# The last attention layer's end: a closing's sum on GpSimd, one row in PSUM, and the last tiles bank by bank

## The chip, the cores and the metric

The kernel runs on one core of a Trainium2 chip. The metric is the device time of one execution, in microseconds. Before the change the median of three runs is 3555.47 us (3555.02 to 3556.88).

Five engines work side by side, each with its own queue: TensorE (PE; its weight loads are listed as PEld), VectorE (DVE), ScalarE (ACT), GpSimd (POOL) and SyncE (SP), which here issues DMAs. PE writes to PSUM; the others work on SBUF, and VectorE and ScalarE on PSUM too.

## The reference

Two graph layers run over `x` (8 batches, 2048 nodes, 256 features) with one 0/1 adjacency matrix. Each is wrapped as `x = layernorm(x + layer(x))`.

```python
# layer 0: per batch, 4 heads of 64; keys in 8 chunks of 256, softmax within a chunk
scores = clip(q @ k / 8, -10, 10); scores = where(adj == 0, -10, scores)
ctx = sum over chunks of softmax(scores) @ v
out = layernorm(ctx @ Wo + bo + x) * gamma + beta
# layer 1: per batch, 4 heads of 64
Wh = h @ W
e = leaky_relu(s_src[i] + s_dst[j], 0.2); e = where(adj, e, -inf)
h_out = elu(softmax(e over j) @ Wh)
```

For layer 1 the kernel uses `max` of two products in place of the exponential of a leaky relu: a tile is `e = max(row_i, gd_j) * edge_ij`, and its product with the values `waug` gives the weighted sums and, in one more column, the denominator. A closing divides by the denominator, applies `elu`, adds the residual and normalizes.

## The kernel before

**Tiling.** All is fp32. Layer 1 of one batch is 128 tiles: 8 units (2 halves of the nodes by 4 heads) of 16 tiles, each tile 128 source nodes by 1024 target nodes. A tile is made by `make` (one VectorE operation, L927) and used by `use` (32 recorded matmuls, L964, into the two PSUM banks of `pa`). For a unit in the last batch with an odd number, both banks of `pa` are one tile, `psA2`.

**Stages.** Layer 1 of batch b runs alongside layer 0 of batch b+1. Two stretches differ. In the *join*, the list `order` at the end of the last batch's loop, the last 20 tiles of batch 6's layer 1 (the held tiles) stand between the last projections of batch 7; the list is written by hand, and each engine gets its queue in that order. `M` is a make, `U` a use, `R` a step of a closing. `b2` and `group.a` are normalizations of the second to last and the last quarter of the nodes; `fs` are four steps that prepare the factors and rows of the next layer 1. `two_banks` hands out three pairs of PSUM banks (`psA0` to `psA2`) in turn.

In the *last layer*, layer 1 of batch 7 runs alone (`self.alone`), 64 steps of two tiles. Every third tile (`by_pool`) is prepared by two ScalarE operations (L888, L889) and one GpSimd product (L890), up to 8 tiles ahead (`make_ahead`); the other two by VectorE. The row that VectorE reads is copied to PSUM by ScalarE (`lift`, L856). A held row still lies in SBUF (`srow`).

**Closings.** When a unit's last tile is used, ScalarE copies `pa` to `raw` (L986), and `close` is stepped along in the following steps: denominators on VectorE (L1005, L1008), the division on GpSimd in the last layer and for the last two units of batch 6 (L1013), Exp and Relu on ScalarE (L1024, L1025), and the sum `min(exp, 1) + relu` on VectorE (L1029), which writes `h1`. The residual of quarters whose heads are all closed is added by GpSimd (L1067, and L1086 for three heads of the last two quarters), VectorE takes statistics (L545, L548), GpSimd raises to the power -0.5 (L556), ScalarE applies (L594).

**The end.** The last unit has no such closing. `Close.last` is a generator of three parts for each of the two last quarters: division, Exp and residual (L1092 to L1099); sum and statistics (L1103, L545); application, alternately on ScalarE and VectorE (L1115, L1118), and the store. The loop at the end steps both generators in turn. For the last `LAST` = 4 tiles the products of bank 0 come first, and those of bank 1 after the fourth tile.

Of the kernel before, what the change touches and what calls it, by code (L numbers as in the profile page):

```python
# [8 lines left out]
F32 = mybir.dt.float32  # L9
# [4 lines left out]
AF = mybir.ActivationFunctionType  # L14
ALU = mybir.AluOpType
AX = mybir.AxisListType

P = 128
# [4 lines left out]
def adj_resnorm_kernel(  # L23
# [19 lines left out]
    nc = tc.nc  # L43
    B, N, F = x.shape
    H, D = a_src.shape
    NT = N // P
    NCH = N // CH
# [24 lines left out]
    UNITS = [(m, h) for m in range(len(BANKS)) for h in range(H)]  # L72
    FIRST = [sum(BANKS[:m]) for m in range(len(BANKS))]
# [3 lines left out]
    WIDE = max(BANKS)  # L77
    AHEAD_E = 5
    AHEAD_P = 8
    ROOMS_P = 5  # L80
    LAST = 4
    n_banks = WIDE // QT
    assert TILES == STEP * SLOTS and NT % 2 == 0 and all(n == WIDE for n in BANKS)

# [8 lines left out]
    psA = ctx.enter_context(tc.tile_pool(name="psA", bufs=1, space=bass.MemoryType.PSUM))  # L93
# [12 lines left out]
        )  # L106
    )

    turn_of, bank_of = [0], [0]

    def two_banks(shape, name):

        turn_of[0] = (turn_of[0] + 1) % 3
        return psA.tile(shape, F32, tag=f"psA{turn_of[0]}", name=name)

    def one_bank(shape, name, kind=F32):

# [6 lines left out]
    h1 = big.tile([P, NT, F], F32, tag="h1", name="h1")  # L124
# [165 lines left out]
    def by_node(dram, b, g):  # L290

        return dram[b, g * CH : (g + 1) * CH, :].rearrange("(t p) f -> p t f", p=P)
# [310 lines left out]
    class Between:  # L603
# [86 lines left out]
    every = tuple(range(QT))  # L690
# [5 lines left out]
    MIDDLE_OF = {  # L696
        1: lambda o: o.bias(),
        5: lambda o: o.g == 0 and o.shift(),
        6: lambda o: o.a.factors(),
        7: lambda o: o.scale(),  # L700
    }
# [9 lines left out]
    NEXT_MIDDLE = {  # L711
        0: lambda o: o.again(),
        3: lambda o: o.b2.factors(),
        4: lambda o: o.load(),
        5: lambda o: o.turn(),
    }
# [80 lines left out]
    class Layer1:  # L797
# [41 lines left out]
        def load_row(self, n):  # L839
            if n < len(UNITS):  # L840
# [9 lines left out]
                )  # L850
                self.rows[n] = srow

        def lift(self, n):
            if n < len(UNITS):
                self.lifted[n] = psA.tile([P, WIDE * P], F32, tag=f"psA{n % 2}", name="rowp")
                nc.scalar.copy(self.lifted[n], self.rows[n])  # L856
# [80 lines left out]
        def use(self):  # L937
# [34 lines left out]

            if self.alone and k >= TILES - LAST:

# [19 lines left out]
        def close(self, u, raw, pas):  # L994
            m, h = UNITS[u]
            n = BANKS[m]

            wide = self.alone and u < len(UNITS) - 2
            if wide:
                yield 1  # L1000
            dn = small.tile([P, n, 1], F32, tag="dn", name="dn")
            if self.alone:
                for i, pa in enumerate(pas):
                    k = slice(i * QT, (i + 1) * QT)
                    nc.vector.tensor_scalar(dn[:, k, :], pa[:, :, D:D1], 1e-30, None, ALU.max)  # L1005
            else:
                nc.vector.tensor_scalar(dn, raw[:, :, D:D1], 1e-30, None, ALU.max)
            nc.vector.reciprocal(dn, dn)  # L1008
            yield 1
            by_pool = self.alone or (self.b == B - 2 and u > len(UNITS) - 3)  # L1010
            if by_pool:
                v = raw[:, :, :D]
                nc.gpsimd.tensor_mul(v, v, dn.to_broadcast([P, n, D]))  # L1013
            for k in range(n):
                if k == n // 2:
                    yield 1
                if not by_pool:
                    v = raw[:, k, :D]
                    nc.scalar.activation(v, v, AF.Copy, scale=dn[:, k, :])  # L1019
            yield 1  # L1020

            ee = small.tile([P, n, D], F32, tag="ee", name="ee")
            hp = raw[:, :, :D]
            nc.scalar.activation(ee, hp, AF.Exp)  # L1024
            nc.scalar.activation(hp, hp, AF.Relu)  # L1025
            yield 1
            if wide:
                yield 1
            nc.vector.scalar_tensor_tensor(  # L1029
                h1[:, FIRST[m] : FIRST[m] + n, h * D : (h + 1) * D],  # L1030
                ee,
                1.0,
                hp,
                op0=ALU.min,
                op1=ALU.add,
            )

        def step(self):
            self.rest(1 + (len(self.tail) > 1))
# [4 lines left out]
    class Close:  # L1044
# [43 lines left out]
        def last(self, pa):  # L1088

            f = slice((H - 1) * D, F)  # L1090
            dn = small.tile([P, QT, 1], F32, tag="dn", name="dn")
            nc.vector.tensor_scalar(dn, pa[:, :, D:D1], 1e-30, None, ALU.max)  # L1092
            nc.vector.reciprocal(dn, dn)
            hh = small.tile([P, QT, D], F32, tag="raw", name="hh")
            nc.vector.tensor_mul(hh, pa[:, :, :D], dn.to_broadcast([P, QT, D]))
            ee = small.tile([P, QT, D], F32, tag="ee", name="ee")
            nc.scalar.activation(ee, hh, AF.Exp)
            hp = small.tile([P, QT, D], F32, tag="acc", name="hp")
            nc.vector.scalar_tensor_tensor(  # L1099
                hp, hh, 0.0, self.x[:, :, f], op0=ALU.max, op1=ALU.add  # L1100
            )
            yield 1
            nc.vector.scalar_tensor_tensor(  # L1103
                self.h[:, :, f], ee, 1.0, hp, op0=ALU.min, op1=ALU.add
            )
            self.n = Norm(self.h, "c")
            self.n.stats(tuple(range(QT)))
            yield 1
            o = self.x
            to = by_node(out, self.b, self.g)  # L1110
            for k in range(QT):
                rs, off = self.n.rs[:, k : k + 1], self.n.off[:, k : k + 1]
                src, dst = self.h[:, k, :], o[:, k, :]
                if k % 2:
                    nc.vector.tensor_scalar(dst, src, rs, off, ALU.mult, ALU.add)  # L1115
                    nc.sync.dma_start(out=to[:, k - 1 : k + 1, :], in_=o[:, k - 1 : k + 1, :])
                else:
                    nc.scalar.activation(dst, src, AF.Identity, bias=off, scale=rs)  # L1118

    HOME = (blocks, "xb", 2)  # L1120
    HOME_Y = (blocks, "y", 2)
# [38 lines left out]
    for g in range(NCH):  # L1160
        _, _, keys, values, queries = groups[g]
# [67 lines left out]
    lower = None  # L1229
    for b in range(B):  # L1230
# [8 lines left out]
        group = before = None  # L1239
        for p in range(PAIRS):  # L1240
# [22 lines left out]
            def hook(now, later):  # L1263
                if group and i in now:
                    now[i](group)
                if before and i in later:
                    later[i](before)
# [3 lines left out]
            if i == 0 and q:  # L1271
                before, group = group, Between(b, q - 1, sd, waug)
# [31 lines left out]
            if ending:  # L1304
                last.bias()
                lower.room = prp, "pr"
            hook(MIDDLE_OF, NEXT_MIDDLE)
            for each in closings:
                each.do(p, "add", "factors")
            if i == 2 and q:  # L1310
# [57 lines left out]
        before = group  # L1368
        gd, fs = factors(b, sd, waug)
        group = None  # L1370
# [8 lines left out]
        coming = Layer1(b, gd, waug)  # L1379
# [33 lines left out]
        if b + 1 < B:  # L1413
            (k0, v0, q0), (l1, t1, k1, v1, q1), (l2, t2, k2, v2, q2), (l3, t3, k3, v3, q3) = turns
            rest = [lambda: lower.rest(1)] if lower else []
            order = [begin, early[0], *rest, l1, k0, ctx, early[2], v0, steps[0], *rest, steps[1], t1, l2, *rest]
            order += [q0, steps[2], early[3], steps[3], l3, k1, *rest, steps[4], v1, early[4], t2, q1]
            order += [steps[5], k2, steps[6], early[5], early[6], steps[7], coming.begin, v2, t3]
            order += [lambda: [load_slab(p) for p in range(2)], steps[8], steps[9]]
            order += [lambda: k3(fs[0]), fs[1], lambda: q2(fs[2]), coming.start, v3, start_next]  # L1420
            order += [lambda: [exps(*us) for us in units_of(0)], q3, coming.make, coming.make]
        else:


            M, U, R = lower.make, lower.use, lambda: lower.rest(1)
            b2 = lambda: before.b2
            order = [begin, U, U, U, ctx, before.again, M, U, lambda: b2().sums(every), steps[1], M]
            order += [lambda: b2().squares(every), lambda: b2().factors(nc.gpsimd), steps[2]]
            order += [lambda: group.a.stats(every), U, U, U, early[2], M, U, M, U, steps[4], before.turn_all]
            order += [lambda: coming.load_masks(0), group_shift, M, U, early[5], early[6], steps[5]]  # L1430
            order += [M, U, R, M, U, R, steps[6], M, U, M, steps[7], U, R, M, M, steps[8], R, M, U, R, M, M]
            order += [steps[9], U, U, fs[0], U, fs[1], fs[2], U, lambda: coming.start(fs[4])]
            assert sum(p is U for p in order) + 1 == LATE * STEP
            assert sum(p is M for p in order) + 2 + 5 >= LATE * STEP
        for piece in order:
# [4 lines left out]
        lower = coming  # L1440
# [17 lines left out]
            each.do(s, "load", "pool", "stats", "most", "finish")  # L1458
    send()
    ends = [ending.of[2 + k].last(pa) for k, pa in enumerate(lower.pa)]  # L1460
    for _ in range(3):
        for end in ends:
            next(end, None)


# [40 lines left out]
```

## Time and profile before

| what | us |
|---|---|
| median of three runs | 3555.47 |
| the profiled execution, its own time | 3554.9 |
| its span, first to last instruction | 3553.1 |
| PE, VectorE, ScalarE, GpSimd busy in the span | 3496.8, 3033.1, 2306.8, 1426.0 |
| first tile of the last layer on PE | 3396.57 |
| last matmul ends | 3539.34 |
| PE busy after 3395, and idle between its instructions | 126.0, 16.8 |

The span is cut from the first to the last instruction; the own time has 1.8 us more around it. A row of a timeline gives start, duration, engine, line, operation, `out<-in`, shapes and a count of equal instructions that follow each other; in square brackets stands how long the engine had been idle, and on what it waited. The mean granted clock of PE is 0.997 of full speed.

### The profile page before, as it was taken

How to read it: one execution, taken by the hardware profiler on the slowest of the kernel's cores; microseconds unless marked ns; L12 is line 12 of the kernel's file. 1: busy time of each engine (PE TensorE's matmuls, PEld its weight loads, DVE VectorE, ACT ScalarE, POOL GpSimd, SP SyncE). 2: the span in 40 equal slices, each digit the busy share in tenths (PEclk: the TensorE clock that was granted, in tenths of full speed). 3: DMA queues.
4: the chain of work that ended last, by engine and by line, in shares of the span. 5: the costliest groups of instructions: out<-in, count | busy, mean ns of one | idle time of the engine just before them, and what ended most of it. 6: DMA issues, size and time to landing. Idle time of an engine off the chain costs nothing. (4 is left out here: it accounts for less than half of the span.)

```text
span 3553.1 us, 170247 instructions
## 1 busy us (share of the span) xinstructions
PE 3496.8 (98%) x76924; PEld 2605.4 (73%) x76924; DVE 3033.1 (85%) x3631; ACT 2306.8 (65%) x4149; POOL 1426.0 (40%) x1264
## 2 busy tenths in 40 slices
PE   8999999999999999999999999999999999999987
PEld 5666677776777777777777767777677776777777
DVE  5886699987999779996899969999699996999888
ACT  4787456655766666665676656766566665766777
POOL 0555233333433334333443333433344333434477
PEclk9999999999999999999999999999999999999999
DMA  7663333443434434434444334444343433434422
GB/s 175 155 134 77 85 103 98 110 96 103 119 104 113 102 104 116 108 102 95 120 117 108 104 83 128 113 110 105 86 128 107 107 101 98 126 109 116 117 92 67
DMA packets 719271, 385.53 MB, mean 109 GB/s; under 512 B 432976, under 2 KB 678608, under 8 KB 718544
## 3 DMA queue, kind: packets, MB, share of 16 engines
q1 hardware_dynamic: 668544, 340.95, 37.4%
q10 hardware_dynamic: 50000, 33.70, 3.0%
q8 instruction: 601, 9.85, 1.1%
q14 instruction: 126, 1.03, 0.1%
HBM read 317.59 MB, written 56.89 MB: 105 GB/s over the span
## 5 line engine op out<-in xcount | busy, mean ns | idle before, releaser
L467 ACT ACTIVATE pr<-pr 128x1024 f32<-128x1024 f32 x956 | 992.2, 1054 | 427.8 <-DVE pr L444 357.6
L444 DVE SCALAR_TENSOR_TENSOR pr<-ps,slab 128x1024 f32<-128x1024 f32 x956 | 1110.4, 1203 | 88.5 <-PE ps L425 79.7
L927 DVE SCALAR_TENSOR_TENSOR e<-srow,gd,et 128x1024 f32<-128x1024 f32 x892 | 1161.3, 1335 | 5.0
L964 PEld LDWEIGHTS pa<-waug,e 128*64 128x64 f32 x32640 | 994.1, 138 | 196.8 <-issue 172.3
L964 PE MATMUL pa<-waug,e 128*64 128x65 f32 x32640 | 1046.6, 223 | 18.2 <-DVE e L927 13.6
L478 PE MATMUL pc<-vaug,pr 128*64 128x65 f32 x30592 | 979.2, 222 | 0.4 <-issue 0.3
L502 POOL TENSOR_TENSOR part<-raw,rd 128x512 f32<-128x512 f32 x446 | 473.6, 1062 | 1216.6 <-DVE rd L495 1212.4
L425 PE MATMUL ps<-qT,kT 64*64 64x512 f32 x8192 | 942.6, 596 | 6.5 <-DVE pr L444 4.1
L478 PEld LDWEIGHTS pc<-vaug,pr 128*64 128x64 f32 x30592 | 936.3, 138 | 14.7 <-DVE pr L444 11.8
L425 PEld LDWEIGHTS ps<-qT,kT 64*64 64x64 f32 x8192 | 287.2, 132 | 483.7 <-issue 270.0
L485 ACT COPY raw<-pc 128x520 f32<-128x520 f32 x512 | 303.0, 592 | 487.2 <-PE pc L478 484.5
L504 POOL TENSOR_TENSOR acc<-acc,part 128x512 f32<-128x512 f32 x446 | 586.1, 1314 | 35.0
L502 POOL TENSOR_TENSOR acc<-raw,rd 128x512 f32<-128x512 f32 x64 | 66.9, 1046 | 361.5 <-DVE rd L495 361.5
L495 DVE RECIPROCAL rd<-raw 128x8 f32<-128x8 f32 x512 | 100.4, 196 | 127.1 <-ACT raw L485 120.3
L673 PE MATMUL pw<-w_sb,x1T 128*64 128x264 f32 (+1 forms) x800 | 122.3, 386 | 2.2 <-ACT x1T L337 2.1
L369 PE MATMUL pp<-xT,wk_sb 128*128 128x512 f32 x256 | 118.5, 603 | 2.9 <-DVE xT L325 1.6
L631 PE MATMUL po<-wo_sb,qT 128*64 128x256 f32 (+1 forms) x912 | 120.2, 379 | 0.0
L369 PE MATMUL pp<-xT,wq_sb 128*128 128x512 f32 x256 | 119.1, 606 | 0.0
L385 PE MATMUL pv<-wv_sb,xT 128*128 128x256 f32 x512 | 116.6, 381 | 0.0
L1019 ACT ACTIVATE sums<-sums,dn 128x64 f32<-128x64 f32 x432 | 112.9, 335 | 0.0
L385 PEld LDWEIGHTS pv<-wv_sb,xT 128*128 128x128 f32 x512 | 95.9, 190 | 20.3 <-issue 7.2
L927 DVE SCALAR_TENSOR_TENSOR e<-rowp,gd,et 128x1024 f32<-128x1024 f32 x87 | 104.9, 1269 | 0.7 <-PE rowp L786 0.7
(170 smaller groups left out, 2562.6 us busy)
## 6 DMA issues: line engine op xcount, KB each, us to landing
et<-edgeD SPq DMA_DIRECT2D x896, 128.0 KB, 2.6
slab<-clipD SPq DMA_DIRECT2D x256, 256.0 KB, 3.7
srow<-rowD SPq DMA_DIRECT2D x252, 128.0 KB, 3.5
x1D<-y ACTq DMA_DIRECT2D x32, 512.0 KB, 2.9
xg<-in_x_dram SPq DMA_DIRECT2D x124, 128.0 KB, 3.2
ctxD<-acc ACTq DMA_DIRECT2D x56, 256.0 KB, 3.6
ctx<-ctxD SPq DMA_DIRECT2D x224, 64.0 KB, 3.0
xp<-in_x_dram SPq DMA_DIRECT2D x224, 64.0 KB, 2.2
```

Source lines behind the costliest of these rows:

```text
L369: nc.tensor.matmul(pps[c], lhsT=w[:, kc, c * P : (c + 1) * P], rhs=st["xT"][:, kc, :], start=(kc == 0), stop=(kc == KC - 1),)
L385: nc.tensor.matmul(pv[:, u, :], lhsT=st["xT"][:, kc, u * P : (u + 1) * P], rhs=wv_sb[:, kc, :], start=(kc == 0), stop=(kc == KC - 1),)
L425: nc.tensor.matmul(ps[z * D : (z + 1) * D, k, :], lhsT=kT[rows, hp, t * P + z * D : t * P + (z + 1) * D], rhs=qT[rows, hp, cols], start=Tr ...
L444: nc.vector.scalar_tensor_tensor(pr, ps, -CLIP, row.unsqueeze(1).to_broadcast([P, 2, CH]), op0=ALU.max, op1=ALU.min,)
L467: nc.scalar.activation(pr, pr, AF.Exp, scale=0.125)
L478: nc.tensor.matmul(pc[z * D : (z + 1) * D, k, to], lhsT=probs[s][u][:, k, i * P + z * D : i * P + (z + 1) * D], rhs=vaug[:, KT * c + u, 2 ...
L485: nc.scalar.copy(raws[s].rearrange("p k i d -> p k (i d)"), pc[:, :, : QT * D1])
L502: engine.tensor_mul(part, raw[:, :, :, :D], rd.to_broadcast([P, 2, QT, D]))
L504: engine.tensor_add(accv, accv, part)
L673: nc.tensor.matmul(pw[z, k, : F + 2 * H], lhsT=self.x1T[:, c, u * P + z.start : u * P + z.stop], rhs=w1_sb[:, c, :], start=(c == 0), stop= ...
L927: nc.vector.scalar_tensor_tensor(e, like(row), self.gd[:, h, j : j + 1], like(self.mask(k)), op0=ALU.max, op1=ALU.mult,)
L964: nc.tensor.matmul(self.pa[i // QT][z * D : (z + 1) * D, i % QT, :], lhsT=block(e, i, z), rhs=self.waug[:, j, h, :], start=(j == 0 and i % ...
```

## The change

Six edits, all in the join, the last layer and the end:

- `close`: where the division is on GpSimd (the last layer, and the last two units of batch 6), the sum is `exp(-relu(-x)) + relu(x)`: two ScalarE passes and a third, and a plain add on GpSimd, in place of the VectorE operation.
- `lift_held` copies the held row to PSUM (`psA0`, name `rowh`); `two_banks` then has only `psA1` and `psA2`.
- In the last pair of the last batch the hook that multiplied by gamma is not called; `before.scale` stands in `order` instead, behind the context transposes and ahead of `before.again`.
- In `order`, one `M` moves from before to behind the statistics of `group.a`, and one `U` from behind `fs[2]` (the rows) to ahead of it.
- `LAST` is 8.
- The generators at the end are stepped in the order 0, 0, 1, 1, 0, 1, and the first of them applies on ScalarE alone.

```diff
-    LAST = 4
+    LAST = 8
...
-    turn_of, bank_of = [0], [0]
+    turn_of, bank_of, turns_of = [0], [0], [0, 1, 2]
 
     def two_banks(shape, name):
 
-        turn_of[0] = (turn_of[0] + 1) % 3
-        return psA.tile(shape, F32, tag=f"psA{turn_of[0]}", name=name)
+        turn_of[0] = (turn_of[0] + 1) % len(turns_of)
+        return psA.tile(shape, F32, tag=f"psA{turns_of[turn_of[0]]}", name=name)
...
+        def lift_held(self):
+
+            n = len(UNITS) - 1
+            t = psA.tile([P, WIDE * P], F32, tag="psA0", name="rowh")
+            nc.scalar.copy(t, self.rows[n])
+            self.rows[n] = t
+
...
-            nc.scalar.activation(ee, hp, AF.Exp)
+            to = h1[:, FIRST[m] : FIRST[m] + n, h * D : (h + 1) * D]
+            if by_pool:
+
+                nc.scalar.activation(ee, hp, AF.Relu, scale=-1.0)
+                nc.scalar.activation(ee, ee, AF.Exp, scale=-1.0)
+            else:
+                nc.scalar.activation(ee, hp, AF.Exp)
             nc.scalar.activation(hp, hp, AF.Relu)
             yield 1
             if wide:
                 yield 1
-            nc.vector.scalar_tensor_tensor(
-                h1[:, FIRST[m] : FIRST[m] + n, h * D : (h + 1) * D],
-                ee,
-                1.0,
-                hp,
-                op0=ALU.min,
-                op1=ALU.add,
-            )
+            if by_pool:
+                nc.gpsimd.tensor_add(to, ee, hp)
+            else:
+                nc.vector.scalar_tensor_tensor(to, ee, 1.0, hp, op0=ALU.min, op1=ALU.add)
...
-                if k % 2:
+                if k % 2 and self.g == NCH - 1:
                     nc.vector.tensor_scalar(dst, src, rs, off, ALU.mult, ALU.add)
-                    nc.sync.dma_start(out=to[:, k - 1 : k + 1, :], in_=o[:, k - 1 : k + 1, :])
                 else:
                     nc.scalar.activation(dst, src, AF.Identity, bias=off, scale=rs)
+                if k % 2:
+                    nc.sync.dma_start(out=to[:, k - 1 : k + 1, :], in_=o[:, k - 1 : k + 1, :])
...
-            hook(MIDDLE_OF, NEXT_MIDDLE)
+            else:
+                hook(MIDDLE_OF, NEXT_MIDDLE)
...
-            order = [begin, U, U, U, ctx, before.again, M, U, lambda: b2().sums(every), steps[1], M]
+            turns_of.remove(0)
+            order = [begin, U, U, U, ctx, lower.lift_held, before.scale, before.again, M, U]
+            order += [lambda: b2().sums(every), steps[1]]
             order += [lambda: b2().squares(every), lambda: b2().factors(nc.gpsimd), steps[2]]
-            order += [lambda: group.a.stats(every), U, U, U, early[2], M, U, M, U, steps[4], before.turn_all]
+            order += [lambda: group.a.stats(every), M, U, U, U, early[2], M, U, M, U, steps[4], before.turn_all]
...
-            order += [steps[9], U, U, fs[0], U, fs[1], fs[2], U, lambda: coming.start(fs[4])]
+            order += [steps[9], U, U, fs[0], U, fs[1], U, fs[2], lambda: coming.start(fs[4])]
...
-    for _ in range(3):
-        for end in ends:
-            next(end, None)
+    for k in (0, 0, 1, 1, 0, 1):
+        next(ends[k], None)
```

## The prediction

> **What bounds the kernel now.** The page comes first: a span of 3553.1 us, TensorE (PE) busy for 98% of it, and a chain whose first long piece starts at 3425.52. Everything that the diff changes runs after 3347 us, so the rest is read from the last stretch alone. First view: busy time of each engine in slices of 20 us. Columns: slice, length, then busy us and instructions for PE, weight loads (PEld), VectorE (DVE), ScalarE (ACT), GpSimd (POOL), then the granted PE clock, the DMA share and GB/s.
>
> ```profile
> 3400.00:3420.00 20.00, 19.92 (x675) 19.64 (x671) 19.85 (x21) 19.76 (x20) 19.67 (x11) 1.00 0.22 70
> 3420.00:3440.00 20.00, 10.26 (x287) 9.84 (x284) 15.87 (x14) 9.21 (x11) 15.31 (x11) 0.74 0.19 63
> 3440.00:3460.00 20.00, 18.98 (x636) 18.56 (x632) 17.95 (x29) 19.04 (x26) 14.87 (x13) 1.00 0.41 122
> 3460.00:3480.00 20.00, 18.19 (x608) 17.91 (x610) 19.85 (x20) 18.72 (x21) 15.13 (x9) 1.00 0.35 108
> 3480.00:3500.00 20.00, 19.30 (x654) 19.03 (x651) 17.73 (x25) 18.06 (x21) 17.95 (x11) 1.00 0.34 98
> 3500.00:3520.00 20.00, 18.93 (x628) 18.46 (x626) 18.17 (x25) 19.52 (x26) 18.22 (x16) 1.00 0.17 57
> ```
>
> All four engines are nearly full, except in 3420 to 3440, where PE does half a slice. The timelines of VectorE and GpSimd show why (start, us, engine, line):
>
> ```profile
> 3414.05 7.19 DVE L927 SCALAR_TENSOR_TENSOR e<-rowp,gd,et 128x1024 f32<-128x1024 f32 x6
> 3425.38 9.72 DVE L1029 SCALAR_TENSOR_TENSOR h<-ee,sums 128x512 f32<-128x512 f32 x1 [4.13 <-ACT sums L1025]
> ...
> 3423.98 2.37 POOL L1067 TENSOR_TENSOR h<-h,kT 128x1024 f32<-128x1024 f32 x1
> 3426.32 3.96 POOL L890 TENSOR_TENSOR e<-e,et 128x1024 f32<-128x1024 f32 x2
> 3430.25 2.34 POOL L1067 TENSOR_TENSOR h<-h,kT 128x1024 f32<-128x1024 f32 x1
> 3432.55 1.99 POOL L890 TENSOR_TENSOR e<-e,et 128x1024 f32<-128x1024 f32 x1
> ```
>
> The closing's sum (L1029), 0.68 us where GpSimd is idle (at 3451.59), took 9.72 us here and ended 0.56 us after GpSimd's row of work. VectorE made no tile for 13.85 us. PE, which needs about 0.97 us a tile (744 records, 32 to a tile, in 22.52 us), stood 8.46 us, then ran until 3438.7 at half its clock.
>
> That is not the only limit. ScalarE's copies of a finished unit (sixteen tiles) stand in its queue behind the products it prepares ahead, and VectorE's next dn, and so its next tiles, wait for these copies:
>
> ```profile
> 3458.51 0.63 ACT L986 COPY sums<-pa 128x260 f32<-128x260 f32 x2
> 3523.19 0.64 ACT L986 COPY sums<-pa 128x260 f32<-128x260 f32 x2
> ```
>
> and in the list of waits (who waited for whom: us in total, times, longest):
>
> ```profile
> DVE dn L1005 <- ACT sums L986: 3.6, 3, 1.9
> ACT ee L1024 <- POOL sums L1013: 8.2, 5, 2.7
> DVE dn L1092 <- PE pa L964: 2.7, 1, 2.7
> ```
>
> I call the copies of unit n S_n. S_2 is at 3458.51; unit 2's last tile, the 48th, left PE at about 3455.7. From S_3 to S_4 and from S_5 to S_6 ScalarE's rows follow each other without a gap.
>
> **The change part by part.** The sum is made against the profiled execution, whose own time is 3554.9 us, 0.57 below the median of 3555.47; the forecast is moved to the median.
>
> *Before the last layer.* The held row's tiles read PSUM, not SBUF. Beside GpSimd, a tile from srow took up to 2.06 us, and the small power operations (L556) 2.04 twice against 1.04 alone, L557 1.45 against 0.20. These are freed; the copy of the row costs ScalarE 1.0 us (L856), in a gap. Moving gamma's product behind the context takes 1.66 us of VectorE waiting and 1.68 us of work away from the context's operands, and GpSimd's sum beside it (2.14) returns to 1.28: context transposes 0.9 earlier. Following the chain (po, statistics, power, apply, x1T), values start 1.6 earlier, the second transposes 1.7, and the row's transposes about 1.45, since the copies of the last held unit now stand before the flat row on ScalarE (0.67 us, paid by the tile that fills PE's 1.09 us wait). The row's store to DRAM goes with it and has over 10 us until its reader. psA has one tag less here, but each reuse waits for a copy that its data needs anyway: nothing. I take 1.4 earlier; bounds 0 (PE's own work hides it) and 2.6 (half of PE's gaps of 1.23, 0.77, 2.14 and 1.09 there).
>
> *The stall.* VectorE loses the 13.85 us, and eight sums of 17.7 us in all. GpSimd gains an add for each, which no row shows: 1.04 (L1013) below, 2.14 (L504 beside a two-input VectorE operation) above. I take 1.25, by L504 alone (1.28) and half of L1067 (1.18), as VectorE no longer reads two SBUF tensors in this stage. But GpSimd is without a gap from 3399 to 3434. Its queue, 1.45 us earlier and with two adds, goes: sums of unit 0 to 3424.3, residual add 3426.65, two tiles 3430.65, residual add 3433.0, closing add 3434.25, tile 3436.25, factors 3438.0, two tiles 3442.0, factors 3443.75, sums of unit 1 to 3444.8. ScalarE now waits for these: from 3420.25 to 3424.3 (ee), then three passes of 0.63, three tiles at 2.22, S_1 at 3432.9, a tile, wait to 3438.0, apply 1.97, tile, row copy to 3443.2, wait to 3444.8, passes 1.9, tile, apply, two tiles: S_2 at 3455.4. Before, it was 3458.5. The add's own new wait, for ScalarE's three passes (done by 3426.2), ends before its turn; behind it stands GpSimd's next tile, which PE reads at about 3436. So of some ten us of stall, 3.1 us are left as gain, 1.45 of them from the start. VectorE also still waits for the residual add before its statistics (ready 3426.65): a new idle of about 4 us, hidden behind ScalarE. With adds at 1.04 or 2.14, S_2 moves by -0.4 or +1.8.
>
> *The third ScalarE pass.* Four closings lie between S_2 and S_6: 4 x 0.64 = 2.6 us on an engine without slack; the waits for PE that fall away (1.02 and 0.25) give back 1.3. S_6 is then 1.8 us earlier, at 3521.4. The last of these adds stands ahead of GpSimd's last two pieces (1.84 each), which end by 3535, before the closings need them.
>
> *Last eight tiles.* After S_6 VectorE makes ten tiles: the first is ready 2.2 us after it (3525.4 before), the tenth nine times 1.185 later, without the sum's 0.68: 3534.3, where it was 3536.73. From there PE before needed half a tile and four second halves, 0.49 + 4 x 0.485 = 2.4 us, which is 3539.3, as measured. Now it needs 0.49 + 8 x 0.485 = 4.4 us: 3538.8. So this edit costs 1.9 us; it would cost 0 if VectorE were well ahead.
>
> *The closings.* VectorE's first dn began at 3539.46, 0.12 us after the last matmul, though bank 0 had ended two us earlier: both banks are one tile, and both closings wait for the whole. The chain of both is still one VectorE queue of 7.3 us. The order moves the first group out sooner, but adds two waits for Exp of about 0.15 us to the second: +0.25. Its four applies on ScalarE (2.1 us) end before the second's factors. If the first closing did start at its bank's end, the second would end 3.4 us sooner: the other bound; above, 0.8 where two-input operations meet the power operation.
>
> Sum: 1.8 + 0.6 - 1.9 - 0.25, or about 0.2 us faster: 3554.7, and 3555.3 on the median's scale.
>
> A rule that speaks against the change: PE's clock fell to 0.5 about 1.3 us after the stall's last matmul and came back some 2.4 us after work began (slices of 2 us show 0.81, 0.50, 0.63, 1.00), costing about half of that; the gaps that ScalarE leaves (4 us before S_2's and S_6's tiles) may do this again, most of it inside PE's slack, at worst 1.4 us between S_2 and S_3, where the slack is least. I take 0. The Trainium skill, TensorE: Matmul & The Clock Gate, Part 1, says that the gate halves the clock after an idle window of about 3.4 us and restores it after as long a busy one; by it two gaps would add an estimated 3.4 us, and the time would be 3558.7. The Trainium skill, SBUF — State Buffer, Who interferes with whom, says that a VectorE operation with two SBUF inputs is blocked by a GpSimd one until that finishes; the 9.72 us, over five GpSimd operations, are longer than one such wait. By the rule alone that sum would have ended about 1.7 us after its start, an estimate; the 1.65 us that the forecast keeps of the stall would be gone, and it would be 3557.
>
> **The rivals.** *ScalarE does not wait* (faster): the three waits of 4.05, 2.3 and 1.6 us vanish if GpSimd is ahead, 3547.3. For it: GpSimd averages 15 to 18 us in later slices. Against: its row from 3399 has no gap.
> *The banks do part* (faster): the first closing runs under the second bank, 3555.3 - 3.4 = 3551.9. For it: that is what two banks allow. Against: the wait of 2.7 above.
> *GpSimd becomes the bound* (slower): adds of 2.14 us delay S_2 by 1.8 and the later factors and sums, which ScalarE's applies wait for, by as much again, with 1.4 for the clock: 3560.3. It decides from about 1.6 us an add. For: L1013 and L504 doubled in the stage before. Against: their partners on VectorE are gone.
>
> **How the numbers follow.** Likeliest 0.62 (3553 to 3557.5); ScalarE free 0.14; banks part 0.10; GpSimd bound 0.14. About 0.2% (7.1 us) is what can be told from no change. Only the first rival's better half, with a better start, passes below 3548.4: 0.12 with other errors; above 3562.6 only GpSimd with everything against it: 0.04. The range takes the bounds (start -1.1, last tiles -1.9, closings -3.4; adds, clock and the rest +5): 3548.5 to 3560.
>
> **What would show it.** No VectorE operation over 2 us after 3400; VectorE tiles of the held unit at about 1.2 us; PE's idle around 3430 in pieces under 5 us; ScalarE over 19 us in the slices to 3520; ee waiting longer for sums; PE's second-bank run of nearly 4 us after the last tile; dn still 0.1 us after the last matmul. The forecast is wrong if the copies at S_2 come before 3450, or if dn starts before PE ends.

## The result, and the profile after

The changed kernel is slower: a median of 3561.33 us (3558.15 to 3564.26, 19 runs) against 3554.94 us (3550.29 to 3558.50, 19 runs) for the kernel before, measured beside it. The ratio is 1.0019, with a 95% interval of 1.0012 to 1.0025, so about 6.4 us. That is within the 0.2% that the prediction took as its bound of "same", but it lies 1.3 us above its range, and the interval does not reach 1. The profiled execution has a span of 3559.3 us and an own time of 3561.19.

The early part of the program, which the change doesn't touch, varies by several us from one execution to the next (in the twelve profiles of this document `pw` begins at 3334.8 to 3342.6). So the stage is compared by distances inside it: from the first of the last projection matmuls (`pw`, L673; at 3336.88 before and 3336.95 after) to the last layer's first tile on PE, then from that tile to each S_n (ScalarE's copies of unit n), to the end of PE, and from there to the end of the span.

| us | before | after | difference |
|---|---|---|---|
| `pw` to the first tile | 59.7 | 58.0 | -1.7 |
| first tile to S_1 | 43.3 | 38.8 | -4.5 |
| first tile to S_2 | 61.9 | 60.9 | -1.0 |
| first tile to S_6 | 126.6 | 132.7 | +6.1 |
| S_6 to the end of PE | 16.2 | 18.0 | +1.8 |
| end of PE to the end of the span | 13.8 | 13.7 | -0.1 |
| `pw` to the end of the span | 216.2 | 222.4 | +6.2 |

So the join gave what it should, S_1 came much earlier, most of that was lost again by S_2, and four units later the kernel was 6.1 us behind. The slices of 20 us, with the columns of the table in the prediction, show the same:

```profile
3400.00:3420.00 20.00, 19.60 (x672) 19.46 (x669) 18.61 (x19) 19.74 (x21) 19.85 (x12) 1.00 0.21 63
3420.00:3440.00 20.00, 14.65 (x426) 14.14 (x424) 12.23 (x28) 14.05 (x19) 19.84 (x15) 0.91 0.19 69
3440.00:3460.00 20.00, 14.73 (x476) 14.59 (x473) 13.16 (x14) 17.11 (x22) 14.39 (x12) 0.92 0.41 127
3460.00:3480.00 20.00, 20.00 (x636) 20.00 (x634) 17.09 (x18) 17.92 (x20) 15.62 (x10) 0.91 0.33 99
3480.00:3500.00 20.00, 19.56 (x662) 19.28 (x657) 15.86 (x24) 17.51 (x22) 17.87 (x11) 1.00 0.37 92
3500.00:3520.00 20.00, 16.53 (x490) 16.02 (x487) 17.13 (x24) 17.01 (x22) 16.67 (x16) 0.91 0.17 57
```

The hole of 3420 to 3440 is smaller (PE 14.65 us, where it was 10.26), but PE now has holes in 3440 to 3460 and in 3500 to 3520 too, VectorE is down to 13.16 us in the first of these, and ScalarE, which was to be full, has 17 to 18 us of work in every slice from 3440 on. Something makes ScalarE wait. The list of waits names it (who waited for whom: us in total, times, longest):

```profile
DVE dn L1012 <- ACT sums L993: 29.2, 7, 8.0
ACT ee L1034 <- POOL sums L1020: 8.5, 4, 3.7
ACT sums L993 <- POOL h L1043: 6.1, 4, 2.8
DVE dn L1101 <- PE pa L971: 5.1, 1, 5.1
```

The third line is new. ScalarE's copies of a unit (L993) wait for GpSimd's add (L1043), which belongs to the closing of the unit before. The copies read `pa` and not what the add writes; but they write `sums`, and the add reads `sums`. That tile has one room (`bufs=1`, L991), so the copies of unit n+1 may not start until the add of unit n has run. The rows of the two engines in this kernel stand end to end:

```profile
3454.58 1.18 POOL L1043 TENSOR_TENSOR h<-ee,sums 128x512 f32<-128x512 f32 x1
3507.07 1.18 POOL L1043 TENSOR_TENSOR h<-ee,sums 128x512 f32<-128x512 f32 x1
3526.46 1.17 POOL L1043 TENSOR_TENSOR h<-ee,sums 128x512 f32<-128x512 f32 x1
```

```profile
3455.79 0.65 ACT L993 COPY sums<-pa 128x260 f32<-128x260 f32 x2 [1.02 <-POOL h L1043]
3508.28 0.65 ACT L993 COPY sums<-pa 128x260 f32<-128x260 f32 x2 [2.82 <-POOL h L1043]
3527.66 0.65 ACT L993 COPY sums<-pa 128x260 f32<-128x260 f32 x2 [1.04 <-POOL h L1043]
```

In front of the add in GpSimd's queue stand tile products (L897) whose input comes from ScalarE (L896). So ScalarE prepares tiles, GpSimd multiplies them, the add follows, and only then may ScalarE copy; behind the copies wait VectorE's `dn` (29.2 us in all, 3.6 before) and all its tiles. The four waits are 1.27, 1.02, 2.82 and 1.04 us. PE, in turn, stands before the tiles behind S_1, S_2, S_5 and S_6 (its timeline):

```profile
3436.08 16.73 PE L971 MATMUL pa<-waug,e 128*64 128x65 f32 x512 [3.60 <-DVE e L934]
3458.08 32.56 PE L971 MATMUL pa<-waug,e 128*64 128x65 f32 x1024 [5.27 <-DVE e L934]
...
3510.64 14.86 PE L971 MATMUL pa<-waug,e 128*64 128x65 f32 x448 [2.22 <-DVE e L934]
3529.95 15.67 PE L971 MATMUL pa<-waug,e 128*64 128x65 f32 x448 [4.45 <-DVE e L934]
```

These gaps cost more than their length. Slices of 2 us around the last one (PE's busy time and records, granted clock, DMA share, GB/s) show the clock:

```profile
3529.00:3531.00 2.00, 1.05 (x20) 0.50 0.00 0
3531.00:3533.00 2.00, 2.00 (x42) 0.50 0.00 0
3533.00:3535.00 2.00, 2.00 (x44) 0.50 0.00 0
3535.00:3537.00 2.00, 2.00 (x72) 0.96 0.04 8
3537.00:3539.00 2.00, 2.00 (x76) 1.00 0.00 0
```

PE came back at 3529.95 and ran at half its clock until about 3535.15, with 42 records in 2 us instead of 76 (a record that reaches over a slice's edge is counted in both slices). What this cost is an estimate: the 448 matmuls are 14 tiles, which take 13.1 us at the 0.93 us a tile worked out further down, and they took 15.67, so some 2.5 us. In "busy" nothing of this shows: a half-speed PE is as busy as a full one.

### The profile page after: what moved, and what is told of

Same layout as the page of the kernel before. It is cut to its first block, busy times and chain, and to the rows that moved or that the text cites. A ratio compares the mean times of both kernels' runs of the same rounds, so it can differ in the third digit from the quotient of the medians.

```text
span 3559.3 us, 170256 instructions
## 1 busy us (share of the span) xinstructions
PE 3501.7 (98%) x76924; PEld 2610.5 (73%) x76924; DVE 3015.1 (85%) x3620; ACT 2312.8 (65%) x4161; POOL 1427.4 (40%) x1273
## 3 DMA queue, kind: packets, MB, share of 16 engines
q14 instruction: 127, 1.04, 0.1%
## 5 line engine op out<-in xcount | busy, mean ns | idle before, releaser
L934 DVE SCALAR_TENSOR_TENSOR e<-srow,gd,et 128x1024 f32<-128x1024 f32 x879 | 1144.3, 1335 | 5.1
L673 PE MATMUL pw<-w_sb,x1T 128*64 128x264 f32 (+1 forms) x800 | 122.3, 387 | 0.5 <-ACT x1T L337 0.5
```

What stands on the lines that cost most here:

```text
L673: nc.tensor.matmul(pw[z, k, : F + 2 * H], lhsT=self.x1T[:, c, u * P + z.start : u * P + z.stop], rhs=w1_sb[:, c, :], start=(c == 0), stop= ...
L934: nc.vector.scalar_tensor_tensor(e, like(row), self.gd[:, h, j : j + 1], like(self.mask(k)), op0=ALU.max, op1=ALU.mult,)
```

## The experiments

My theory after the result: the copies' wait for the one room of `sums` is what made the stage longer (T1). The rivals: the third pass on ScalarE is dearer than assumed (T2); the adds and their own waits make GpSimd the bound (T3); the last eight tiles and the closings' order cost it (T4). T1 was formed on the trace, after the prediction, which had none of it. The kernel before was timed again beside each group of runs: 3556.68 us beside the first four below, 3552.05 beside the next three, 3555.09 beside the last three. So times of different groups are compared by their ratios to it, and each run's distances come from one profiled execution.

**Two rooms for `sums` in the last layer.** The add and everything else stay.

```diff
-                raw = small.tile([P, WIDE, D1], F32, tag="sums", name="sums", bufs=1)
+                if self.alone:
+                    raw = blocks.tile([P, WIDE, D1], F32, tag="xb", name="sums")
+                else:
+                    raw = small.tile([P, WIDE, D1], F32, tag="sums", name="sums", bufs=1)
```

> The changed kernel, with the closing's `sums` tile of the last layer in two buffers (in rooms of `blocks` that are free by then) in place of one. Theory (a new wait): ScalarE's copies of a finished unit write the one `sums` tile that GpSimd's add of the unit before still has to read, and that add stands in GpSimd's queue behind tiles which wait for ScalarE; the changed kernel's profile has 6.1 us of ScalarE idle on this wait, 2.8 of it ahead of the sixth unit's copies. Then the wait is gone, the last unit's copies come 3 to 6 us sooner (3527.7 in the changed kernel) and the time is 3555.5 to 3558.5. Rival (load): ScalarE's third pass and GpSimd's add are the cost themselves, and the wait only stands where ScalarE would be late anyway: 3560 to 3562, with the wait turned into one for GpSimd's sums or PE.

Measured: 3555.65 us (3554.24 to 3561.24, 11 runs), 0.9998 of before [0.9990, 1.0007]. By the two ratios to before that is some 7 us less than after. The execution that was profiled is the longest of the eleven, since its `pw` comes 5.7 us later than in after; from `pw` to the end it takes 216.8 us instead of 222.4. In the timeline of ScalarE the copies now follow the row before them without a gap:

```profile
3507.74 1.13 ACT L895 ACTIVATE e<-srow,ngd 128x1024 f32<-128x1024 f32 x1
3508.91 1.15 ACT L896 ACTIVATE e<-e,gd 128x1024 f32<-128x1024 f32 x1
3509.97 0.63 ACT L996 COPY sums<-pa 128x260 f32<-128x260 f32 x2
...
3527.28 1.15 ACT L896 ACTIVATE e<-e,gd 128x1024 f32<-128x1024 f32 x1
3528.34 0.63 ACT L996 COPY sums<-pa 128x260 f32<-128x260 f32 x2
```

S_2 to S_6 takes 67.9 us instead of 71.9 (before: 64.7), and PE ends 145.2 us after the first tile instead of 150.7. So the one room cost 5.5 us at the end of PE: 1.1 up to S_2, 4.0 from S_2 to S_6, where the waits of 2.82 and 1.04 stood, and 0.5 behind S_6. From S_2 to S_6 3.2 us more than before are left. T3, as adds that take too long, falls too: they take 1.17 to 1.19 us, and ScalarE's wait for GpSimd's division is 8.5 us in after and 8.2 before. T1 is itself a wait for GpSimd's queue, though, and no run shortens that queue alone. VectorE's `dn` still waits 24.4 us for the copies, since these still stand in ScalarE's queue behind the tiles prepared ahead.

**The closing's sum back on VectorE.** One Exp, then the sum on VectorE, as before; all else as after.

```diff
-            if by_pool:
-
-                nc.scalar.activation(ee, hp, AF.Relu, scale=-1.0)
-                nc.scalar.activation(ee, ee, AF.Exp, scale=-1.0)
-            else:
-                nc.scalar.activation(ee, hp, AF.Exp)
+            nc.scalar.activation(ee, hp, AF.Exp)
...
-            if by_pool:
-                nc.gpsimd.tensor_add(to, ee, hp)
-            else:
-                nc.vector.scalar_tensor_tensor(to, ee, 1.0, hp, op0=ALU.min, op1=ALU.add)
+            nc.vector.scalar_tensor_tensor(to, ee, 1.0, hp, op0=ALU.min, op1=ALU.add)
```

> The changed kernel with the closing's sum back on VectorE and Exp as one pass; the join, the last eight tiles and the order of the end stay changed. Theory (the sum's move costs): the long VectorE sum beside GpSimd is back (about 9 us at its worst place), yet the time falls, by the wait for GpSimd's add (6.1 us of ScalarE idle) and the third pass (about 4 us), to 3554 to 3557. Rival (the rest costs): the moved sum is worth its stall, and the loss lies in the last eight tiles and the end; then the time rises to 3565 or more.

Measured: 3557.12 us (3552.61 to 3560.04, 11 runs), 0.9998 of before [0.9989, 1.0007]. The stall is back, in the same place and of the same length (VectorE's timeline):

```profile
3411.81 7.19 DVE L934 SCALAR_TENSOR_TENSOR e<-rowp,gd,et 128x1024 f32<-128x1024 f32 x6
3422.47 9.73 DVE L1037 SCALAR_TENSOR_TENSOR h<-ee,sums 128x512 f32<-128x512 f32 x1 [3.47 <-ACT sums L1033]
```

S_1 and S_2 are at 43.5 and 61.9 us after the first tile, as before the change (43.3 and 61.9). So moving the sum does take the stall away, and with it 4.7 us at S_1; of these only 1.0 is left at S_2 with one room of `sums` and 2.1 with two. That ScalarE's waits for GpSimd eat most of the stall's length was the prediction's reading, and it fits. PE ends 146.4 us after the first tile, 4.3 less than in after: so much the move of the sum cost in all. Of the 3.6 more than before that are left, 1.9 lie behind S_6 (18.02 and 16.15 us), where this kernel has eight last tiles and PE its full clock, and 1.7 lie ahead of it. S_2 to S_6 took 66.4 us here, 1.7 more than before, although the closings are those of before; the difference lies between S_2 and S_3 (16.7 us, 14.9 before), where ScalarE waited 2.66 us for unit 3's last tile instead of 1.02. Why PE is later there wasn't settled; its clock was 1.00.

**Four last tiles instead of eight.**

```diff
-    LAST = 8
+    LAST = 4
```

> The changed kernel with four tiles held back at the end, not eight. Theory (as forecast): the last tile from VectorE sets the end, and eight second halves behind it are four too many: PE ends 1.9 us sooner after VectorE's last tile (5.0 us in the changed kernel, about 3 here), and the time is 3559 to 3560. Rival: PE is behind VectorE there, and the time is the same, 3561 to 3562.

Measured: 3562.81 us (3560.92 to 3565.22, 11 runs), 1.0015 of before [1.0006, 1.0023]. PE ends 150.5 us after the first tile (150.7 with eight). The two rows behind S_6 say why: PE's 448 matmuls and VectorE's ten tiles.

```profile
3531.34 15.54 PE L971 MATMUL pa<-waug,e 128*64 128x65 f32 x448 [4.45 <-DVE e L934]
```

```profile
3530.05 11.96 DVE L934 SCALAR_TENSOR_TENSOR e<-rowp,gd,et 128x1024 f32<-128x1024 f32 x10
```

VectorE's last tile is ready at 3542.01, PE ends at 3546.88. PE is slower than VectorE here, because of its clock, and has all its work left whatever the order of the banks. So in this kernel going back to four tiles gains nothing, and T4 does not explain the loss by the eight tiles.

**The two banks of the last unit as two tiles.**

```diff
-                if self.alone and n % 2:
+                if self.alone and n == len(UNITS) - 1:
+                    self.pa = [
+                        psA.tile([P, QT, D1], F32, tag=f"psA{2 - 2 * i}", name="pa")
+                        for i in range(n_banks)
+                    ]
+                elif self.alone and n % 2:
```

> The changed kernel, with the last unit's two banks as two tiles (the second in the pair of banks of the row that is no longer read), so that each of the two last closings waits for its own bank. Theory (as forecast): in the changed kernel both wait for the last matmul, since both banks are one tile; apart, the first dn starts about 3.9 us ahead of PE's end, the second closing is alone behind it, and the time from PE's end to the end falls from 13.7 us by 3 to 3.5: 3557.5 to 3558.5. Rival: the wait is not by the tile, or GpSimd and the stores set the end: less than 1 us.

Measured: 3558.11 us (3554.90 to 3563.21, 11 runs), 1.0004 of before [0.9995, 1.0013]. VectorE's first `dn` after its last tile, in after and then in this kernel:

```profile
3545.74 0.16 DVE L1101 TENSOR_SCALAR dn<-pa 128x4 f32<-128x4 f32 x1 [5.12 <-PE pa L971]
```

```profile
3541.71 0.16 DVE L1106 TENSOR_SCALAR dn<-pa 128x4 f32<-128x4 f32 x1 [1.38 <-PE pa L976]
```

In after it starts 0.12 us behind the last matmul and has waited 5.12 us; here it starts 3.61 us ahead of the last matmul, and the tail from the end of PE to the end of the span is 10.0 us instead of 13.7. That the whole tile was waited for is so shown: with the new order and the eight tiles in place, parting the banks is worth 3.7 us in the tail (3.2 from `pw` to the end, since PE ended 0.5 later); with the banks as one tile the tail was only 0.1 shorter than before.

**Both of these together.** Two rooms for `sums`, and the banks apart.

> The changed kernel with both mends: two buffers for the last layer's `sums` tile, and the last unit's two banks as two tiles. The two act at different places (copies of the units, and the end after the last matmul), so theory says that they add: 5.6 and 3.7 us by the two profiles, 3551.5 to 3553.5, faster than the kernel before. Rival: they overlap, or part of the first was chance: 3554 to 3556.

Measured: 3552.18 us (3550.10 to 3556.51, 11 runs), 1.0006 of before [0.9998, 1.0015]. In the profile `pw` to the end is 213.9 us, 8.4 less than after: 5.6 at the end of PE and 3.7 in the tail, less 0.9 of a later first tile (PE's clock was 0.50 ahead of it, and 1.00 in after). Against before it is 2.3 us less. So in the profile the gains add. The timed runs do not show it: the median lies in the expected range only because the kernel before ran 4.6 us faster in this group, and the ratio is no lower than that of two rooms alone (0.9998). The change is back to even, and a gain over the kernel before isn't shown.

**Every fourth tile by ScalarE and GpSimd, not every third.** On top of the kernel just shown. It asks whether ScalarE's queue sets the pace of the stage, and takes nine tiles (41 to 32) off ScalarE; it takes them off GpSimd too.

```diff
         def by_pool(self, k):
-            return self.alone and k % 3 == 2 and k > 2
+            return self.alone and k % 4 == 3
...
-                if t // 3 % ROOMS_P < 3:
+                if t // 4 % ROOMS_P < 3:
```

> The kernel with both mends, and every fourth tile of the last layer (not every third) prepared by ScalarE and GpSimd, the others by VectorE: 32 tiles in place of 41 or 42. Theory (ScalarE sets the pace of the last layer): it loses some 20 us of work, VectorE gains about 11 (1.185 us a tile) and becomes the bound at about 126 us; from the last layer's first tile to the last matmul it takes 130 to 137 us, where it took 145 with two buffers, and the time is 3539 to 3546. Rival (GpSimd's and VectorE's queues or PE set the pace just as much): the time is within 2 us of the kernel with both mends.

Measured: 3541.88 us (3540.48 to 3544.15, 11 runs), 0.9973 of before [0.9964, 0.9982]. PE ends 135.4 us after the first tile, 9.7 less than in the kernel above and 7.4 less than before. The list of waits of the last layer has turned round:

```profile
ACT sums L1001 <- PE pa L976: 13.6, 5, 3.7
DVE dn L1020 <- ACT sums L1001: 7.2, 7, 2.8
PE pa L976 <- DVE e L934: 4.9, 6, 1.4
```

ScalarE now waits for PE and is ready for the copies; VectorE's `dn` waits 7.2 us in all, not 25.4 as in the kernel above; PE's longest wait for a VectorE tile is 1.4 us, and its clock stays at 1.00 in every slice from 3420 to 3520. VectorE makes more tiles and is busy for 18 to 20 us of each of those slices, so it may well be the next limit. Whether ScalarE's queue or GpSimd's had set the pace this edit doesn't part; that GpSimd waited 19.3 us for ScalarE's tiles in after, and 14.9 before, speaks for ScalarE's.

**The end's edits alone, in the kernel before.** Eight last tiles, the new order of the closings, the first one's applies on ScalarE, and the banks apart; nothing else of the change. The apply's edit is that of the change; the rest:

```diff
-    LAST = 4
+    LAST = 8
...
-    for _ in range(3):
-        for end in ends:
-            next(end, None)
+    for k in (0, 0, 1, 1, 0, 1):
+        next(ends[k], None)
```

> The kernel before with the end alone changed: eight tiles held back, the closings one behind the other, and the last unit's banks as two tiles. Theory: the order of the end is worth 3 to 4 us once the banks are two tiles, since the first closing then lies beside the second bank's matmuls; VectorE's last tile comes shortly before PE's end there, so eight tiles held back cost up to 1.9 of it: 1.5 to 3.5 us faster than the kernel before. Rival: something else at the end (GpSimd's powers, the stores) holds it, or the eight tiles cost all of it: within 1 us of the kernel before.

Measured: 3552.43 us (3544.73 to 3558.82, 11 runs), 1.0003 of before [0.9994, 1.0011]. In the profile the end of PE is 1.5 us later than before (144.25 and 142.77 from the first tile), and the tail 3.5 us shorter: 2.0 us together, which the runs can't tell from nothing. VectorE's last tile is at 139.8, 0.4 earlier than before, so the price of eight tiles where PE has its full clock is 1.9 us: from S_6 to the end of PE it takes 18.01 us, not 16.15. The sum on VectorE took 9.71 us in the same place.

**Without the clamp.** On top of the kernel with two rooms and banks apart, the three passes are one Exp and one Relu, and GpSimd's add stays. The clamp of the exponential at 1 is left out, so what is computed is not `elu`; only the time of the third pass is looked at.

```diff
-                nc.scalar.activation(ee, hp, AF.Relu, scale=-1.0)
-                nc.scalar.activation(ee, ee, AF.Exp, scale=-1.0)
+                nc.scalar.activation(ee, hp, AF.Exp)
```

> The kernel with both mends (two buffers, banks apart), with the added ScalarE pass left out: the kernel leaves out the clamp of the exponent at zero, so that GpSimd adds exp(x) and relu(x), which is not elu where x is positive. Theory: ScalarE has no slack between the third unit's copies and the last but one's, so a pass of 0.64 us less per closing brings these copies 2.6 us closer (68.0 us with the pass), and the last matmul 3 to 4 us nearer to the last layer's first tile (145.1 with it). Rival: the pass lies in waits, less than 1 us. One look; read from the distances inside the last layer.

Measured: 3549.77 us in one run, so the distances count. S_2 to S_6 takes 66.2 us instead of 68.0, PE ends 142.5 us after the first tile instead of 145.1. The third pass costs 1.8 us over these four closings, less than the 2.6 of its own length, and 2.6 in the whole stage, where 3 to 4 were expected. The one room cost 5.5, so T2 falls as the main cause; it is the second one.

**Two variants of every fourth tile.** One with `LAST = 4`:

```diff
-    LAST = 8
+    LAST = 4
```

> The kernel with every fourth tile prepared by ScalarE and GpSimd, with four tiles held back in place of eight. VectorE sets the end there and PE keeps its full clock. Theory: four second halves fewer stand behind VectorE's last tile, PE ends 1.4 to 1.9 us sooner; but the first closing then has less to lie beside, and gives back up to 1.9: the time is within 1 us of that with eight. Rival: the eight tiles only cost: 1.5 to 2 us faster.

One where GpSimd's tiles begin with the eighth instead of the fourth, since PE waited 2.00 us for the fourth:

```diff
-            return self.alone and k % 4 == 3
+            return self.alone and k % 4 == 3 and k > 3
```

> The kernel with every fourth tile prepared by ScalarE and GpSimd, with tile 3 on VectorE, so that the first such tile is tile 7. PE waited 2.0 us for tile 3 (GpSimd's first product). Theory: the wait goes and VectorE pays 1.2 us for one more tile, which it has not to spare later: 0.5 to 2 us faster. Rival: VectorE is the bound throughout and the tile costs it all back: the same, within 0.5 us.

Measured: 3541.35 us (3536.82 to 3542.67, 5 runs), 0.9961 of before [0.9948, 0.9974], and 3541.56 us (3540.06 to 3542.01, 5 runs), 0.9963 [0.9949, 0.9977]. Neither can be told from every fourth tile alone. In the profile the first has S_6 to the end of PE 16.0 us, not 17.9, and gives the gain back in the tail (11.9 us instead of 10.0). The second has no wait of 2.00 us and its copies 1.4 us earlier from S_0 to S_2, but only 0.8 of it is left at the end of PE, and, as its first tile came 0.8 later behind `pw`, nothing at the end of the span (203.3 us from `pw` in both). Nor can that wait be put down to the fourth tile's engine alone: the first variant leaves that tile to GpSimd and had no such wait either. In both variants PE's clock was 0.50 for the first tiles of the last layer (28 records in 3396 to 3398 in the first variant), while it was 1.00 with every fourth tile; a slower PE came to the fourth tile later.

## Why the prediction was wrong

**The start.** Right. The first tile came 58.0 us after `pw` instead of 59.7, which is 1.7 earlier where 1.4 was forecast.

**The stall and GpSimd's queue.** Right to 0.8 us or better up to S_2. The division of unit 0 ended at 3423.94 (forecast 3424.3), the adds took 1.17 to 1.19 us (1.25), `ee` waited 3.65 us for it (4.05), VectorE's statistics 3.67 us for the residual add ("about 4"), S_1 was at 3433.72 (3432.9) and S_2 at 3455.79 (3455.4). VectorE had no operation above 2 us from 3400 on. The rival "ScalarE does not wait" falls with these waits. The rival "GpSimd becomes the bound" rested on adds of 2.14 us, and falls; that its 3560.3 is the nearest of all forecasts is luck. But both S_1 and S_2 already contained a wait of over 1 us for the add, which nothing in the forecast had; other small errors covered it, and that S_2 agrees to 0.4 us is luck too: without these waits, with two rooms, it comes 1.1 us sooner.

**The step that failed: S_6 at 3521.4** ("The third ScalarE pass"). It was 3527.66, 6.3 us later. Its error stands a paragraph earlier, in "The add's own new wait, for ScalarE's three passes (done by 3426.2), ends before its turn; behind it stands GpSimd's next tile, which PE reads at about 3436". It asked what the add waits for and what stands behind it on GpSimd. It didn't ask who waits for the add. The add reads a tile with one room, so the next writer of that tile waits for it. While the sum stood on VectorE, it had long read `sums` when the next copies came; on GpSimd it stood behind tile products that depend on ScalarE itself. Two rooms took away 5.5 us at the end of PE and, by the ratios, some 7 us of the time: shown by that run. From S_2 to S_6 the forecast had 66.0 us and after took 71.9; the room accounts for 4.0 of the 5.9 missed. As to the rest, the paragraph let 1.3 us of waits for PE fall away, but ahead of S_3's copies ScalarE waited 1.86 us for PE, where it had been 1.02. The pass cost 1.8 us net, not 1.3; and without the pass, with two rooms, S_2 to S_6 still takes 66.2 us, 1.5 more than before, which stays open.

**The clock.** Taken as nothing, with "at worst 1.4". Measured: behind four gaps PE's clock was 0.50 while it worked for 3.4, 5.4, 3.4 and 5.2 us (from the slices of half a us shown below). Behind S_6 that cost some 2.5 us, by the estimate above, and set the end of PE; but the 1.8 us by which after was slower there than before are not the clock's alone, since at full clock the eight last tiles cost 1.9 by themselves. Behind S_2 it lies partly in slack (S_3's copies waited 1.9 us for PE). The forecast also read the clock's return in the kernel before too early: slices of half a us have 0.50 until 3439.5, not 3438.7. The forecast asked only of the gaps of some 4 us that it foresaw; the copies' waits made one of 5.27 us and added one of 2.22, and that one too was enough, so the gaps of the failed step are what brought the clock down. The estimate by the skill's page, 3558.7, was nearer than the sum, though for a part of the loss only.

**"PE needs about 0.97 us a tile."** Nearly right, and not what bounds the stage. In the row of 1024 records above, 32 tiles take 32.56 us, the first 5.39 of them at half clock, which leaves an estimated 0.93 us a tile at full clock. That is 119 us for 128 tiles, where the stage took 142.8 us before, 150.7 after, and 135.4 with every fourth tile. A page that has PE busy for 98% doesn't show this room.

**The last eight tiles.** The term of 1.9 us did not show in after: PE, at half clock, was behind VectorE by more than the order of the banks can cost. Where the clock was full it measured 1.9 us each time, from S_6 to the end of PE: 18.01 against 16.15 in the kernel before with the end's edits, 17.88 against 16.01 with every fourth tile. The mechanism and the size were right for the situation that the forecast had in mind, and that did not come.

**The closings.** Right: `dn` 0.12 us behind the last matmul, since the banks are one tile. The order cost -0.1 us, not +0.25. The rival "the banks do part" falls for this change, and its price of 3.4 us was right (3.7 when they were parted).

**ScalarE.** The reading that ScalarE's queue, and not the stall, sets the pace fits all runs, though every fourth tile relieved GpSimd too, and explains why removing a stall of 9.7 us brought so little. It should have been followed one step further, to all that ScalarE would come to wait for.

**The range.** Its own terms add up to 3548.9 and 3560.3, not to 3548.5 and 3560; that changes nothing here.

What stays open: the 1.5 us named above; why unit 3 ended later with the sum on VectorE (1.7 us), and whether the end's edits and the parted banks, or two rooms with them, beat the kernel before; the profiles say 2 us, the runs can't tell. What does beat both kernels is every fourth tile on ScalarE and GpSimd, with two rooms and parted banks: 3541.88 us, 0.9973 of before.

## What to carry to other kernels

When an operation moves to another engine, ask not only what it will wait for, but who waits until it has read: every tile that it reads with a single room ties the tile's next writer to the new engine's queue, and two rooms were the cure here. Before a stall is removed, look at which engine's queue sets the pace behind it; here taking nine tiles from ScalarE and GpSimd was worth some ten us and the stall's end one or two. And in a stage with gaps, look at the time per tile in an unbroken row of matmuls and at the clock that the profile grants, not at PE's busy time.

## What the hardware showed that was not expected

- PE's clock goes by a grid. In slices of half a us of the changed kernel (PE's busy time and records, granted clock, DMA share, GB/s) the clock falls and comes back at these places:

```profile
3436.00:3436.50 0.50, 0.42 (x8) 0.66 0.00 0
3439.50:3440.00 0.50, 0.50 (x22) 0.93 0.04 10
3456.50:3457.00 0.50, 0.00 (x0) 0.64 0.54 186
3463.00:3463.50 0.50, 0.50 (x15) 0.53 0.51 152
3511.00:3511.50 0.50, 0.50 (x22) 0.75 0.78 266
3514.50:3515.00 0.50, 0.50 (x20) 0.83 0.78 262
3528.00:3528.50 0.50, 0.00 (x0) 0.82 0.00 0
3535.00:3535.50 0.50, 0.50 (x20) 0.85 0.16 33
```

  With 1.00 on the one side and 0.50 on the other, the share of each gives the moments: 3436.16 to 3439.57, 3456.64 to 3463.47, 3511.25 to 3514.67, 3528.32 to 3535.15. The spells last 3.41, 6.83, 3.42 and 6.83 us, and their starts lie 20.48, 54.61 and 17.07 us apart, 6, 16 and 5 times 3.413. The Trainium skill, TensorE: Matmul & The Clock Gate, Part 1, gives such a free-running window of 3413 ns, and the trace agrees. The page's idle window of that length is not what it took here: at 3508.41 to 3510.64 PE was idle for 2.22 us, and was busy for 1.2 us of the 3.41 that end at 3511.25, and still the clock fell for one window. Behind the gaps of 5.27 and 4.45 us it stayed low for a second window, though PE had worked for 2.0 and 1.8 us of the first. Nor does the grid start with the program: in after, two rooms, four last tiles, banks apart, every fourth tile and the run without the clamp the last layer's first tile came 57.96 to 58.00 us after `pw`, and in three more kernels with the same code up to there 58.8 to 59.0, with a clock of 0.50 in the slices just ahead of it. So a difference of 1 us between two profiles can be the clock's place on its grid.
- VectorE's sum behind five GpSimd operations in a row took 9.72, 9.73 and 9.71 us in three kernels; it is no chance of one profile. The Trainium skill, SBUF — State Buffer, Who interferes with whom, has the one that issues first hold the shared ports for its whole instruction while the other is blocked; the measured wait lasted over several GpSimd instructions.
- In the join, where the held row moved to PSUM, the small GpSimd power operations (L556) took 1.01 us twice instead of 2.04 twice, and L557 0.20 and 0.23 instead of 1.45 and 0.59. They ran beside VectorE's tiles both times, which read the row from SBUF before and from PSUM after; L557's 1.45 also ran beside an addition with two SBUF inputs (L619). So reads from SBUF by VectorE seem to hold up GpSimd's 128x4 operations too; no run parts this from the other edits in the join.
